# Two-layer graph network, layer 1: the exponential part of ELU taken as exp(-relu(-z)) on ScalarE and added by an accumulating DMA; the sum S1 of u formed by an accumulating load

## The chip, the cores and the metric

The kernel runs on one core of one Trainium2 chip. The metric is the device time of one execution in microseconds (us). The profile covers one execution; its span runs from the first to the last instruction of the core.

## The reference

16 graphs share one adjacency matrix of 1024 x 1024; each node has 512 features. Everything is float32.

```python
# layer 0
h = maximum(layernorm(x), 0)
x = x + (adj @ h) @ weight + bias                 # per graph
# layer 1
u = maximum(layernorm(x), 0)
h = u @ W
s1, s2 = h @ a[:512], h @ a[512:]
e = leaky_relu(s1[:, None] + s2[None, :], 0.2) * adj
att = softmax(e, axis=1)
x = x + elu(att @ h + beta * h)
```

elu(z) is max(z, 0) + min(exp(z), 1) - 1. Since min(exp(z), 1) = exp(min(z, 0)), it is also max(z, 0) + exp(-relu(-z)) - 1. The constant -1 is already in the stored residual x1, so a kernel adds relu and the exponential to x1 and nothing more.

## The kernel before

**Layers and batches.** Layer 0 is computed for the 16 graphs (the code calls them batches) one after another, then layer 1 for the 16. Layer 0 leaves three things of each batch in DRAM: the residual x1 (`x1d`, in four quarters by node half and by q), the normalised u (`ud`, tiles U00, U01, U10, U11) and the vectors for the logits. Layer 1 first forms z = p u, where p is the unnormalised softmax with beta on its diagonal, then multiplies by W (the tiles pq), and scales by 1/sum (`rs`) inside the ELU.

**Seven products.** Each 2 x 2 block product is done in seven products with sums of blocks (p1 to p7). S1, S2 and S4 are such sums on the left side; for layer 1 they are made from the four U tiles by `left_half`, called by `u_sums` in two parts: part 0 makes S1 (the sum of the right halves of U0q and U1q) and S2 = S1 - A11, part 1 makes S3 and S4. In layer 1 the second multiplication runs in the order p1, p5, p2, p6, p7, p3, p4 (`P5_EARLY`), each product in two halves q = 0, 1 of eight matmuls, in six PSUM banks: X (p5, p3), Y (p1, p6, p7, p4) and W (p2). p1's steps lie between the steps of the first multiplication's p4.

**The ELU.** When a product is finished, `done` copies or reads its bank. p6 and p5 are copied to z tiles by ScalarE (`part`); p7 and p3 are added to them by VectorE (`rest`), and then `elu` follows. p2 and p4 go to `elu` straight from PSUM. `elu(nh, oh, q, ...)` has `parts` (ScalarE: Relu into the output tile o, Exp into ez; each for two rows of 256 columns) and `total` (VectorE: o += min(ez, 1)). For p3 and p4 `total` is followed by a GpSimd DMA that adds x1 from DRAM to o, and `store` writes o out by SP's queue. ez is the z tile itself for p7 and p3, a tile of its own for p2 and p4; ez, z and the three `ext` tiles of the first multiplication's p4 share tag b2, which has five slots. o has tag xp with four slots, the U and S tiles tag up with seven.

**Order of the work.** Every instruction keeps its program order on its engine, and the same holds for the DMA queues of SP and GpSimd (POOL). Work beside the matmuls is placed by hand: plans map a step number k to functions. In the first multiplication step k comes after each half product (a step is 3.4 us) and k = 12 to 18 are the steps of its p4; in the second, k = 2n + q for product number n (1.7 us), to 13. What falls due later goes into the dictionary `later`, and a key over 13 becomes step key - 14 of the next batch. In layer 1 the softmax of the next batch runs beside the current batch: `masked` (M0 to M7, ScalarE and VectorE), `spread_max` (X, x: the row maxima out to DRAM and back, tiles md and mall, by SP), `top` (N, n), `exp` (E0 to E7, ScalarE), `turn` (V0 to V7, VectorE), `spread_sum` (S, s), `diagonal` (D, d). In batches 1 to 8 one row of batch 15's layer-0 output is also finished (`late`). In the profile nearly all lines are L119, that of the helper that keeps program order, so groups are told apart by tiles.

Of the kernel before, what the change touches and what calls it, by code (L numbers as in the profile page):

```python
# [29 lines left out]
F32 = mybir.dt.float32  # L30
AF = mybir.ActivationFunctionType
# [35 lines left out]
def kernel(  # L67
# [474 lines left out]
    def h_relu(b, k):  # L542
        h_norms.pop((b, k)).relu()

    def left_half(k, a11, a12, a21, a22, s, parts=(0, 1)):

        s1, s2, s4 = (s[n][:, ts(k, 2), :] for n in ("S1", "S2", "S4"))
        if 0 in parts:
            add(s1, a21, a22)
            add(s2, s1, a11, ALU.subtract)  # L550
        if 1 in parts:
            add(a21, a11, a21, ALU.subtract)
            add(s4, a12, s2, ALU.subtract)

    def h_sums(b, k):
        h1, h2 = hs[b, 0], hs[b, 1]
# [164 lines left out]
    def load_u(b, names):  # L721
        for n in names:
            t = uts.setdefault(b, {})[n] = up.tile([P, 2, D], F32, tag="up", name=f"ul_{b}_{n}")
            sp.dma_start(out=t.rearrange("p k d -> p (k d)"), in_=ud[b][n])

    def u_sums(b, q, part):
        t = uts[b]
        if q == 0 and part == 0:
            for n in ("S2", "S1", "S4"):
                t[n] = up.tile([P, HC, HD], F32, tag="up", name=f"ul_{b}_{n}")  # L730
        u1, u2 = t[f"U0{q}"], t[f"U1{q}"]
        left_half(q, u1[:, :, 0:HD], u2[:, :, 0:HD], u1[:, :, HD:D], u2[:, :, HD:D], t, (part,))

    def u_blk(b, n, k):
        t = uts[b]
# [6 lines left out]
    class Softmax:  # L742
# [9 lines left out]

        def logits(self):
            b = self.b
            self.rs = stat.tile([P, NCH], F32, tag="rs", name=f"rs_{b}")
            self.s1b = stat.tile([P, G, NCH], F32, tag="s1b", name=f"s1b_{b}", bufs=1)
            self.s2b = stat.tile([P, SN], F32, tag="s2b", name=f"s2b_{b}", bufs=1)
            for s in range(G):
                sp.dma_start(
                    out=self.s1b[ts(s, Q)], in_=s1d[b].rearrange("(t r) g -> r t g", r=Q)  # L760
                )
                sp.dma_start(
                    out=self.s2b[ts(s, Q)], in_=s2d[b][s, 0:SN].partition_broadcast(Q)
                )
# [92 lines left out]
        def diagonal(self, h):  # L857
            sz = stat.tile([P, 2, HC], F32, tag="sz", name=f"sz_{self.b}_{h}")
            dve.tensor_reduce(
                out=sz[:, 0, :], in_=self.half[h]["sall"].rearrange("p t i -> p i t"),  # L860
                axis=AX.X, op=ALU.add,
            )
            dve.reciprocal(self.rs[:, ts(h, HC)], sz[:, 0, :])
            dve.tensor_scalar(sz[:, 1, :], sz[:, 0, :], beta_c, None, op0=ALU.mult)
            for i in range(HC):
                d = self.t[f"B{h + 1}{h + 1}"][:, i, ts(i, P)]
                dve.scalar_tensor_tensor(
                    d, ident, sz[:, 1, i : i + 1], d, op0=ALU.mult, op1=ALU.add
                )
# [40 lines left out]
    def layer1(b, plan_a, plan):  # L910

        rs = sms[b].rs
        rows = node_rows(out, b)
        end = b == B - 1
        zs = {}
        sums = {}

        def elu(nh, oh, q, z, k):

            if end:  # L920
                r = b4.tile([P, 2, HD], F32, tag="b4", name=f"r_{b}_{nh}{oh}{q}")
            else:
                if (nh, q) not in sums:
                    sums[nh, q] = xp.tile([P, 2, D], F32, tag="xp", name=f"o_{b}_{nh}{q}")
                r = sums[nh, q][:, :, ts(oh, HD)]
            g0 = HC * nh + 2 * q
            ez = zs.pop((nh, oh, q), None)
            if ez is None:
                ez = b2.tile([P, 2, HD], F32, tag="b2", name=f"ez_{b}_{nh}{oh}{q}")

            def parts():
                for i in range(2):
                    sc = rs[:, g0 + i : g0 + i + 1]
                    act.activation(r[:, i, :], z[:, i, :], AF.Relu, scale=sc)
                    act.activation(ez[:, i, :], z[:, i, :], AF.Exp, scale=sc)

            if end or ez is not z:
                parts()
            else:
                later.setdefault(k + 1, []).append(parts)  # L940
            full = x1s[b, nh, q] if end else sums[nh, q]

            def total():
                d = full[:, :, ts(oh, HD)]
                if end:
                    add(d, d, r)
                dve.scalar_tensor_tensor(d, ez, 1.0, d, op0=ALU.min, op1=ALU.add)
                if nh != oh and not end:
                    pool.dma_start(
                        out=full.rearrange("p k d -> p (k d)"), in_=x1d[b][nh, q],  # L950
                        accum_op=ALU.add,
                    )

            def store():
                for s in range(G):
                    (act if end and nh and s % 2 else sp).dma_start(
                        out=rows[s][:, ts(2 * nh + q, 2), :], in_=full[ts(s, Q)]
                    )

            later.setdefault(k + (1 if end else 2 if ez is not z else 3), []).append(total)  # L960
            if nh != oh:
                later.setdefault(k + (1 if end else 7), []).append(store)

        products = NODES_LAST if end else P5_EARLY
        at = {p[0]: 2 * n for n, p in enumerate(products)}
        weighted1 = []

        def part(nh, oh, q, ps):
            zs[nh, oh, q] = b2.tile([P, 2, HD], F32, tag="b2", name=f"z_{b}_{nh}{oh}{q}")
            act.copy(zs[nh, oh, q], ps)  # L970

        def rest(nh, oh, q, ps, k):
            z = zs[nh, oh, q]
            add(z, ps, z)
            elu(nh, oh, q, z, k)

        def done(prod, q, ps):
            if prod == "p1":
                weighted1[0].fork("W", q, ps)
            elif prod == "p6":  # L980
                part(0, 1, q, ps)
            elif prod == "p5":
                part(1, 1, q, ps)
            elif prod == "p7":
                rest(1, 1, q, ps, at[prod] + q)
            elif prod == "p3":
                rest(0, 1, q, ps, at[prod] + q)
            else:
                elu(0 if prod == "p2" else 1, 0, q, ps, at[prod] + q)

        def after(k):
            for f in later.pop(k, ()):
                f()
            beside(plan)(k)

        weighted1.append(Weighted(f"pq{b}", w1_c, done, products))
        pT = sms[b].t

        def p4_operands():
            return partial(u_inner, b), p4_sums.pop(b), pT["T4"], p4_ext.pop(b)  # L1000

        beside(plan_a)(-1)
        left = products_a(
            f"z{b}", lambda n, k: u_blk(b, n, k), lambda n, k: pT[n][:, k, :], beside(plan_a),
            FORKED, p4=(p4_operands, weighted1[0]),
        )
        weighted1[0].rest(1, left, after)
# [77 lines left out]

    def logit_weights(k):

        v = stat.tile([P, DC], F32, tag="v", name=f"v_{k}")
        for dc in range(DC):
            dve.tensor_tensor_reduce(  # L1090
                out=junk(1), in0=w1_t[:, dc, :], in1=v_bcs[k], scale=1.0, scalar=0.0,
                op0=ALU.mult, op1=ALU.add, accum_out=v[:, dc : dc + 1],
            )
        vd[k] = dram.tile([D], F32, name=f"vd_{k}")
        sp.dma_start(out=vd[k].rearrange("(c p) -> p c", p=P), in_=v)
# [137 lines left out]
    for b in range(B):  # L1233
        plans = [plan_out(out_of, b)] if b else []
        plans_b = []
        if b + 1 < B:
            if b:
                plans.append(steps((-1, load_x, b + 1, 0), (-1, load_x, b + 1, 1)))
            plans.append(plan_norm_a(b + 1))
            out_of = LayerOut(b)  # L1240
            plans_b += [
                steps(
                    (11, out_of.stats, 0, 0, 0), (11, out_of.keep, 0, 0),
                    (12, out_of.stats, 0, 0, 1), (12, out_of.stats, 0, 1),
                ),
                plan_norm_b(b + 1), plan_softmax(EARLY_B.get(b, {}), sms[0]),
            ]
        else:
            plans.append(plan_softmax(FIRST_A, sms[0]))
            plans.append({  # L1250
                22: [(load_u, 0, ("U00", "U01"))], 25: [(load_u, 0, ("U10", "U11"))],
            })
            plans_b += [
                plan_softmax(FIRST_B, sms[0]), plan_softmax(LOGITS_B, sms[1]),
            ]
        if 0 < b <= G:
            plans.append({23: [(store_mask, b - 1)]})
# [22 lines left out]
    for b in range(B):  # L1280
# [24 lines left out]
            if b == NCH:  # L1305
                plan_b[13].append((late.store_logits,))
        if b + 1 < B:
            plan_b = merged(plan_b, steps((10, u_sums, b + 1, 0, 0), (12, u_sums, b + 1, 1, 0)))
        plans.append({18: plan_b.pop(1, [])})
        layer1(b, merged(*plans), plan_b)  # L1310
    for k in sorted(later):
# [35 lines left out]
```

## Time and profile before

| | |
|---|---|
| median of three runs | 2257.12 us (2254.89 to 2257.17) |
| the profiled execution's own time | 2254.63 us |
| its span | 2252.7 us |
| PE busy | 2236.1 us, 99% |
| VectorE busy | 1950.3 us, 87% |
| ScalarE busy | 1547.9 us, 69% |
| GpSimd busy | 243.7 us, 11% |
| DMA moved | 336.07 MB |

PE is TensorE's matmuls, ACT is ScalarE, DVE is VectorE, POOL is GpSimd, SP the queue of most DMAs. An instruction line in a timeline has its start, its duration, engine, line, operation, output <- inputs, shapes, count, and in brackets the idle time of the engine ahead of it and what ended it. A window's line has the busy time of each engine in that stretch, with the number of instructions in parentheses.

### The profile page before, as it was taken

The page shows a single profiled execution, that of the slowest core. Times are in us where ns is not written, and L with a number is a line of the kernel's source. Part 1 is how long each engine was busy: PE and PEld are TensorE (multiplying, and loading weights), DVE is VectorE, ACT ScalarE, POOL GpSimd, SP SyncE. Part 2 cuts the span into 40 slices and gives each one's busy share as a digit, 9 for nine tenths or more (in the row PEclk, how much of TensorE's full clock was granted, in tenths as well). Part 3 has the DMA queues.
Part 4 walks back from the last instruction along what each step waited for, and adds up shares of the span by engine and source line. Part 5 has one row for each costly group of instructions (what it writes and reads, how often), then busy time and mean ns, then how long its engine had stood idle before and what let it go on. Part 6 is the DMA issues. An engine that isn't in the chain of part 4 may idle for free.

```text
span 2252.7 us, 30436 instructions
## 1 busy us (share of the span) xinstructions
PE 2236.1 (99%) x8716; PEld 1645.5 (73%) x8716; DVE 1950.3 (87%) x4477; ACT 1547.9 (69%) x4138; POOL 243.7 (11%) x508
## 2 busy tenths in 40 slices
PE   9999999999999999999999999999999999999998
PEld 5888888888888888888666556665666556665565
DVE  7888888998888998898989988898889988888864
ACT  3766766676777676776576777768777776767743
POOL 1211111111111111111000000000000000000000
PEclk9999999999999999999999999999999999999999
DMA  7433454443444343344535665465554655446541
GB/s 210 140 126 119 160 171 132 141 140 117 148 160 151 134 142 120 120 150 159 202 110 175 165 169 166 145 196 156 164 168 149 191 142 153 139 143 165 159 120 49
DMA packets 194296, 336.07 MB, mean 149 GB/s; under 512 B 78800, under 2 KB 86992, under 8 KB 194128
## 3 DMA queue, kind: packets, MB, share of 16 engines
q1 hardware_dynamic: 185168, 302.15, 41.2%
q0 software_dynamic: 8640, 31.46, 7.5%
q8 instruction: 68, 1.11, 0.2%
q14 instruction: 100, 0.82, 0.1%
q10 hardware_dynamic: 320, 0.52, 0.1%
HBM read 228.33 MB, written 109.91 MB: 150 GB/s over the span
## 4 chain that ended last, share of the span: by engine, by line
PE 96%; DVE 2%; ACT 1%; DMA 1%; issue 0%; POOL 0%; SPq 0%; DVEq 0%; POOLq 0%
PE z_Y L119 16%; PE po_Y L119 10%; PE pq_Y L119 9%; PE z_X L119 9%; PE y_Y L119 8%; PE po_X L119 5%; PE z_W L119 5%; PE pq_X L119 5%; PE y_X L119 4%; PE y_W L119 3%; PE y_p7y L119 2%; PE pq_W L119 2%; PE po_W L119 2%; PE z_p4y L119 2%; PE y_p3y L119 2%; PE y_p4y L119 2%
## 5 line engine op out<-in xcount | busy, mean ns | idle before, releaser
L119 ACT ACTIVATE e<-e,nm 128x256 f32<-128x256 f32 x480 | 236.8, 498 | 51.4 <-DVE nm L119 51.4
L119 DVE CUSTOM_DVE_ANT_0 e<-e,mask 128x256 f32<-128x256 f32 x512 | 199.9, 424 | 54.0 <-ACT e L119 52.8
L119 PE MATMUL z_Y<-pT,ul_U 128*128 128x512 f32 x512 | 224.9, 592 | 0.0
L119 ACT ACTIVATE e<-s2b,s1b 128x256 f32<-128x256 f32 x512 | 214.7, 500 | 0.0
L119 PE MATMUL pq_Y<-w_c,z_C 128*128 128x256 f32 x768 | 189.1, 379 | 0.0
L119 PE MATMUL po_Y<-w_c,y_C 128*128 128x256 f32 x768 | 188.3, 379 | 0.0
L119 PEld LDWEIGHTS z_Y<-pT,ul_U 128*128 128x128 f32 x512 | 97.3, 190 | 115.6 <-issue 111.5
L119 DVE CUSTOM_DVE_ANT_0 y_S<-xr,v_bc 128x512 f32<-128x512 f32 x240 | 165.3, 689 | 9.2 <-DVE s L119 0.5
L119 PEld LDWEIGHTS po_Y<-w_c,y_C 128*128 128x128 f32 x768 | 145.9, 190 | 20.3 <-ACT po_X L119 0.2
L119 PEld LDWEIGHTS pq_Y<-w_c,z_C 128*128 128x128 f32 x768 | 145.9, 190 | 19.9
L119 DVE STREAM_TRANSPOSE pT<-e 128x512 f32<-128x512 f32 x240 | 150.8, 680 | 1.5
L119 ACT ACTIVATE h<-h,nb_h,r_h 128x512 f32<-128x512 f32 (+1 forms) x132 | 98.2, 792 | 57.1 <-POOL nb_h L119 57.1
L119 ACT ACTIVATE y_S<-xr 128x512 f32<-128x512 f32 x90 | 56.7, 630 | 91.9 <-DVE xr L119 91.5
L119 POOL DMA_DIRECT2D o<-x1d x60 | 52.7, 935 | 609.7 <-DVE o L119 546.8
L119 PE MATMUL pq_X<-w_c,z_S 128*128 128x256 f32 x512 | 115.9, 379 | 0.0
L119 PE MATMUL po_X<-w_c,y_S 128*128 128x256 f32 x512 | 115.7, 379 | 0.0
L119 PE MATMUL z_W<-pT,ul_U 128*128 128x512 f32 x256 | 112.5, 592 | 0.0
L119 PE MATMUL z_Y<-pT_T,ul_S 128*128 128x512 f32 x256 | 112.5, 592 | 0.0
L119 PE MATMUL z_X<-pT_T,ul_S 128*128 128x512 f32 x256 | 112.5, 592 | 0.0
L119 PE MATMUL z_X<-pT,ul_S 128*128 128x512 f32 x256 | 112.5, 592 | 0.0
L119 PEld LDWEIGHTS pq_X<-w_c,z_S 128*128 128x128 f32 x512 | 96.3, 190 | 14.5 <-DVE z_C L119 0.8
L119 PEld LDWEIGHTS po_X<-w_c,y_S 128*128 128x128 f32 x512 | 97.3, 190 | 13.2
(259 smaller groups left out, 5238.3 us busy)
## 6 DMA issues: line engine op xcount, KB each, us to landing
mask<-maskd SPq DMA_DIRECT2D x128, 512.0 KB
h<-in_x_dram SPq DMA_DIRECT2D x64, 512.0 KB
xr<-in_x_dram SPq DMA_DIRECT2D x256, 128.0 KB
x1d<-xr SPq DMA_DIRECT2D x64, 512.0 KB
ul_U<-ud_U SPq DMA_DIRECT2D x64, 512.0 KB
ud_U<-xr SPq DMA_DIRECT2D x60, 512.0 KB
o<-x1d POOLq DMA_DIRECT2D x60, 512.0 KB, 8.0
out_dram<-o SPq DMA_DIRECT2D x240, 128.0 KB
```

Source lines behind the costliest of these rows:

```text
L119: return lambda *args, **kwargs: tc.keep_in_program_order(f(*args, **kwargs))
```

## The change

In batches 0 to 14 of layer 1, `parts` makes ez with two Relu of scale -1/sum (a second half of `rs` that GpSimd fills) and one Exp of scale -1 over 512 columns in place. Two DMAs on GpSimd's queue follow from `parts` itself: o += ez, and for p3 and p4 o += x1. VectorE's `total` and its place in `later` go. The last batch keeps Exp, `total` and its steps. S1 of each batch is no longer added by VectorE: `load_s1` has SP load the right half of U0q from DRAM and GpSimd's queue add that of U1q, at step 2 of the batch before (for batch 0 at step 5 of layer 0's last batch). The tag of a small tile used once (`v`) is shared with another.

```diff
+    def load_s1(b):
+        s1 = up.tile([P, HC, HD], F32, tag="up", name=f"ul_{b}_S1")
+        uts.setdefault(b, {})["S1"] = s1
+        for i, queue in ((0, sp), (1, pool)):
+            for q in range(2):
+                queue.dma_start(
+                    out=s1[:, ts(q, 2), :],
+                    in_=ud[b][f"U{i}{q}"].rearrange("p (k d) -> p k d", d=D)[:, :, HD:D],
+                    **({"accum_op": ALU.add} if i else {}),
+                )
...
     def u_sums(b, q, part):
...
-            for n in ("S2", "S1", "S4"):
+            for n in ("S2", "S4"):
...
-        left_half(q, u1[:, :, 0:HD], u2[:, :, 0:HD], u1[:, :, HD:D], u2[:, :, HD:D], t, (part,))
+        if part == 0:
+            add(t["S2"][:, ts(q, 2), :], t["S1"][:, ts(q, 2), :], u1[:, :, 0:HD], ALU.subtract)
+        else:
+            left_half(q, u1[:, :, 0:HD], u2[:, :, 0:HD], u1[:, :, HD:D], u2[:, :, HD:D], t, True)
...
-            dve.reciprocal(self.rs[:, ts(h, HC)], sz[:, 0, :])
+            dve.reciprocal(self.rs[:, 0, ts(h, HC)], sz[:, 0, :])
+            pool.tensor_scalar(
+                self.rs[:, 1, ts(h, HC)], self.rs[:, 0, ts(h, HC)], -1.0, 1.0, op0=ALU.mult,
+                op1=ALU.mult,
+            )
...
+            full = x1s[b, nh, q] if end else sums[nh, q]
+
             def parts():
                 for i in range(2):
-                    sc = rs[:, g0 + i : g0 + i + 1]
-                    act.activation(r[:, i, :], z[:, i, :], AF.Relu, scale=sc)
-                    act.activation(ez[:, i, :], z[:, i, :], AF.Exp, scale=sc)
+                    c = slice(g0 + i, g0 + i + 1)
+                    act.activation(r[:, i, :], z[:, i, :], AF.Relu, scale=rs[:, 0, c])
+                    if end:
+                        act.activation(ez[:, i, :], z[:, i, :], AF.Exp, scale=rs[:, 0, c])
+                    else:
+                        act.activation(ez[:, i, :], z[:, i, :], AF.Relu, scale=rs[:, 1, c])
+                if end:
+                    return
+                act.activation(ez, ez, AF.Exp, scale=-1.0)
+                pool.dma_start(out=r, in_=ez, accum_op=ALU.add)
+                if nh != oh:
+                    pool.dma_start(
+                        out=full.rearrange("p k d -> p (k d)"), in_=x1d[b][nh, q],
+                        accum_op=ALU.add,
+                    )
...
             def total():
                 d = full[:, :, ts(oh, HD)]
-                if end:
-                    add(d, d, r)
+                add(d, d, r)
                 dve.scalar_tensor_tensor(d, ez, 1.0, d, op0=ALU.min, op1=ALU.add)
-                if nh != oh and not end:
-                    pool.dma_start(
-                        out=full.rearrange("p k d -> p (k d)"), in_=x1d[b][nh, q],
-                        accum_op=ALU.add,
-                    )
...
-            later.setdefault(k + (1 if end else 2 if ez is not z else 3), []).append(total)
+            if end:
+                later.setdefault(k + 1, []).append(total)
...
-            plan_b = merged(plan_b, steps((10, u_sums, b + 1, 0, 0), (12, u_sums, b + 1, 1, 0)))
+            plan_b = merged(plan_b, steps(
+                (2, load_s1, b + 1), (10, u_sums, b + 1, 0, 0), (12, u_sums, b + 1, 1, 0)
+            ))
```

More of the change, by code (lines that the diff above doesn't have):

```diff
@@ L543, in h_relu, with left_half @@
         h_norms.pop((b, k)).relu()
-    def left_half(k, a11, a12, a21, a22, s, parts=(0, 1)):
+    def left_half(k, a11, a12, a21, a22, s, rest=False):
         s1, s2, s4 = (s[n][:, ts(k, 2), :] for n in ("S1", "S2", "S4"))
-        if 0 in parts:
+        if not rest:
             add(s1, a21, a22)
             add(s2, s1, a11, ALU.subtract)
-        if 1 in parts:
-            add(a21, a11, a21, ALU.subtract)
-            add(s4, a12, s2, ALU.subtract)
+        add(a21, a11, a21, ALU.subtract)
+        add(s4, a12, s2, ALU.subtract)
     def h_sums(b, k):
@@ L754, in logits @@
             b = self.b
-            self.rs = stat.tile([P, NCH], F32, tag="rs", name=f"rs_{b}")
+            self.rs = stat.tile([P, 2, NCH], F32, tag="rs", name=f"rs_{b}")
             self.s1b = stat.tile([P, G, NCH], F32, tag="s1b", name=f"s1b_{b}", bufs=1)
@@ L940, in elu @@
                 later.setdefault(k + 1, []).append(parts)
-            full = x1s[b, nh, q] if end else sums[nh, q]
             def total():
                 d = full[:, :, ts(oh, HD)]
-                if end:
-                    add(d, d, r)
+                add(d, d, r)
                 dve.scalar_tensor_tensor(d, ez, 1.0, d, op0=ALU.min, op1=ALU.add)
-                if nh != oh and not end:
-                    pool.dma_start(
-                        out=full.rearrange("p k d -> p (k d)"), in_=x1d[b][nh, q],
-                        accum_op=ALU.add,
-                    )
             def store():
@@ L1086, in logit_weights @@
     def logit_weights(k):
-        v = stat.tile([P, DC], F32, tag="v", name=f"v_{k}")
+        v = stat.tile([P, DC], F32, tag="bn", name=f"v_{k}")
         for dc in range(DC):
@@ L1254 @@
                 plan_softmax(FIRST_B, sms[0]), plan_softmax(LOGITS_B, sms[1]),
+                steps((5, load_s1, 0)),
             ]
```

## The prediction

> **What bounds the kernel now.** I read the busy shares first, then who keeps TensorE waiting, then one batch of layer 1 engine by engine.
>
> ```profile
> PE 2236.1 (99%) x8716; PEld 1645.5 (73%) x8716; DVE 1950.3 (87%) x4477; ACT 1547.9 (69%) x4138; POOL 243.7 (11%) x508
> 1314.29:1385.75 71.46, 71.46 (x237) 44.70 (x237) 62.95 (x158) 51.92 (x149) 5.32 (x8) 1.00 0.59 166
> 1110.00:1160.00 50.00, 48.76 (x157) 29.35 (x156) 47.37 (x115) 32.99 (x104) 0.00 (x0) 1.00 0.43 145
> ```
>
> The second and third lines are windows (length, then busy time of PE, PEld, DVE, ACT, POOL, then clock, DMA share, GB/s). A layer-1 batch takes 71.4 us and PE is busy in all of it; VectorE has 8.5 us to spare in a batch, ScalarE 19.5. In layer 1 only batch 0 (third line) shows PE idle, 1.24 us. The other idle time of PE, 16.6 us in all, is 4.2 us in the first 25 us, 10.0 us in the last 63, and about 1 us elsewhere; the change touches neither end. So work taken from VectorE can return about 1 us, and the question is only whether the new path makes PE wait. The matmul spans are modelled, but their starts are regular: 16 of 256 columns every 3.45 us, all through layer 1. What PE needs, and when, stands in the timeline of batch 3:
>
> ```profile
> 1368.32 3.62 PE L119 MATMUL pq_W<-w_c,z_C 128*128 128x256 f32 x16
> 1371.77 3.62 PE L119 MATMUL pq_Y<-w_c,z_S 128*128 128x256 f32 x16
> 1375.22 3.62 PE L119 MATMUL pq_Y<-w_c,z_C 128*128 128x256 f32 x16
> 1392.45 7.03 PE L119 MATMUL z_W<-pT,ul_U 128*128 128x512 f32 x16
> ...
> 1370.29 0.47 ACT L119 ACTIVATE o<-pq_W,rs 128x256 f32<-128x256 f32 x1 [1.19 <-DMA s2b<-s2d]
> 1373.70 0.59 ACT L119 COPY z<-pq_Y 128x512 f32<-128x512 f32 x1
> 1375.42 0.59 ACT L119 COPY z<-pq_Y 128x512 f32<-128x512 f32 x1 [1.14 <-PE pq_Y L119]
> 1378.30 0.51 ACT L119 ACTIVATE o<-z,rs 128x256 f32<-128x256 f32 x1 [2.29 <-DVE z L119]
> 1382.70 0.81 ACT L119 ACTIVATE late<-late,nb_u,r_u 128x512 f32<-128x512 f32 x1 [0.54 <-POOL nb_u L119]
> 1390.06 0.61 ACT L119 COPY z_W<-z_Y 128x512 f32<-128x512 f32 x1
> ```
>
> p2, p6 and p7 of the weighted product follow one another; p6 and p7 accumulate in the same two Y banks, so p7's second half (8 matmuls on, 1376.95) must wait for ScalarE's copy of p6's second half, which ends at 1376.01: **0.94 us of slack**. The copy into z_W ends at 1390.67 and p2 of the next batch uses it at 1392.45: **1.78 us of slack** where a late batch-15 row is handled (b = 1 to 8), 2.66 us where not (1817.72 + 0.57 against 1820.95). These are the two places where ScalarE can stop PE.
>
> **What the skill says.** "DMA: Bandwidth & Descriptors", SWDGE vs HWDGE vs iDMA: accumulation is possible from GpSimd's queue alone. The trace agrees: o<-x1d, the one accumulating transfer, is POOL's. The same page, Anatomy of one DMA — SWDGE (gpsimd) path, prices one at 2.0 us plus bytes over 436 GB/s: 3.2 us for 512 KB, 2.6 us for 256 KB. The trace differs:
>
> ```profile
> 1388.00 0.91 POOL L119 DMA_DIRECT2D o<-x1d  x1 [5.33 <-DVE o L119]
> DMA to landing us min/median/max: 5.6/5.6/5.6
> o<-x1d POOLq DMA_DIRECT2D x60, 512.0 KB, 8.0
> ```
>
> The one issued at 1388.00 runs alone on idle DMA engines and lands after 5.6 us; all 60 have a median of 8.0. The trace decides. Queues, rings and completion order: an engine with several rings turns between them packet by packet; here the transfers that overlap mask loads are the long ones (9.4 us for that of 1395.46), which agrees. "ScalarE: Activation LUTs", Table sets: relu is in exp's set; the profile has one table load in the whole span, so no reload is charged.
>
> **The change, part by part** (batches 0 to 14 of layer 1; the last keeps its code).
>
> *VectorE.* Eight scalar_tensor_tensor of 0.69 us a batch go (the groups o<-ez,o and o<-z,o, 120 in all), and two S1 adds of 0.68 us: 6.9 us a batch, some 103 us in all. PE covers it wholly: gain 0 to 1.2 us, taken as 0.
>
> *ScalarE.* Each of eight parts keeps four 128x256 instructions (Exp becomes Relu, both near 0.47 to 0.51 us) and gets one Exp of 128x512 in place. No row has it. From 256 to 512 columns a PSUM copy goes from 0.37 to 0.586 us, so 0.50 for an Exp of 256 gives 0.71; back to back the spans overlap by 0.1, so 0.62 of queue time. Bounds: 0.5 and 0.8 (the scaled 128x512 row of xr). That is 5.0 us a batch beside 19.5 idle: it matters only ahead of the two copies.
>
> *The wait for the slot (step 1).* Tag b2 has five slots. When p6's second half is to be copied out, z of p5 (two tiles, in use until p7) and z of p6's first half are held, and so are both ez of p2. Before, the sixth tile took the slot of p2's first ez as soon as VectorE had read it (1373.67 to 1374.36). Now that slot is free only when the DMA r += ez has landed. From PE's end of p2's first half (1370.2): 0.1 to ScalarE, 1.57 for four Relu, 0.13 for the wait on its own result, 0.71 for Exp, 0.1 to POOL, then the landing L, 0.1, the copy 0.59, 0.1 to PE: 3.4 + L. PE wants it 6.75 us after 1370.2. So PE stalls L - 3.35. L for 256 KB in 1 KB pieces has no row: alone, first packet 1.6 us after issue (as at 1388.00), half of the 2.6 us of packets, and the 1.4 left of the 5.6: 4.3. Four mask loads (2 MB, issued from 1370.6) share the engines until 1378; the contended 512 KB takes 1.4 to 3.8 us longer than the lone one. I take L = 6.5, bounds 4.2 and 9.4. Stall 3.15 us, bounds 0.85 and 6.05; times 15 batches: **47 us** (13 to 91). Behind the waiting copy on ScalarE stand p7's parts, which wait for VectorE's add anyway.
>
> *ScalarE's lag at z_W (step 2).* After that stall ScalarE begins p7's first part 1.5 us late, PE is 3.15 late. Six parts add 6 x 0.62 = 3.7 us, of which ScalarE's old 0.54 and part of its 2.29 us wait absorb some; the late row's POOL steps now stand behind the DMA issue of p7's first part (0.9 us). Worked through, the z_W copy lands some 1.1 us past its need in eight batches and 0.3 in seven: **11 us**. If step 1 is short the absorption goes and this grows to 1.8 and 0.9, 21 us; with a long one it is nothing.
>
> *POOL and SP (step 3).* POOL gets eight r DMAs and two S1 DMAs a batch at 0.9 us of issue, and two small tensor_scalar (0.3 us). For p3 and p4 it waits, in order, for r to land before it may issue o += x1d; the next half's r stands behind. With landings of 4 to 8 us this is a chain of four links, about 28 to 35 us from p3's first part to the last landing, where before four transfers went out within 7.5. SP waits for each with its stores, and behind the third store is the second max exchange (md, then mall), at 1414.96 before. By my times that is issued about 4 us later, with PE 4 us later too: 0 taken. ScalarE has no idle time between 1413.84 and 1431, and the p4 copies in it have about 1.2 us to spare, so each us beyond that stops PE: bounds 0 and 4 us a batch, 60 us.
>
> *S1 by transfer.* Two SP loads (0.4 us each to issue, ahead of the logit and mask loads, which have 20 us before their use) and two accumulating ones which wait for them on POOL. Issued about 1364, landed about 1374; VectorE uses S1 at 1381.2. Cost 0; if it were 5 us late VectorE's 8.5 us of idle, now 15, covers it. Its packets are done before p2's r DMA starts; if not, L takes it up.
>
> **Sum.** 2254.6 us is the profiled execution's own time (its span 2252.7, with 1.9 around it). 47 + 11 + 0 = 58 gives 2312.6; the median is 2.5 us above that execution, so 2315.
>
> **Rivals.**
> (B) *POOL's chain decides as well*: landings of 8 us or more put the second max exchange over 1.2 us behind PE. For it: the median of 8.0, and SP already waited 8.6 us at most for a small md transfer. Against: the four o += x1d no longer run on top of each other. 2 to 4 us more in 15 batches: 2345 to 2375.
> (C) *Short landing*: L about 4.3, stall 0.95, and the z_W lag of 1.8 and 0.9: 15 x 0.95 + 21 = 35, so 2292. Against: the mask loads at that moment.
> (D) *Not slower*: the transfer is hidden at p6's second copy. It decides at L = 3.35 us; below that PE sees nothing there, and if ScalarE's extra Exp costs under 0.3 us a part (1.78 over six) z_W is in time too: 2256, about 1 us under. Against: a first packet at 1.6 us and 1.4 us to land leave 0.35 for the packets. That the change should not do what it says I see no way for: the two VectorE groups are gone from the code.
>
> **Numbers.** 0.2% is about 4.5 us, what a measurement of this kernel can tell from no change. Forecast (A) 0.52, B 0.25, C 0.15, D 0.08, of which 0.05 within 0.2% and 0.03 faster. A alone spans 2295 to 2345; the range takes in C's lower bound (13 + 11) and B: 2278 to 2380.
>
> **What would show it.** Right: PE idle ahead of p7's second half in each of 15 batches, released by ScalarE's z copy, that copy waiting for a DMA on o; a smaller one at z_W; 120 Exp of 128x512 near 0.71 us; VectorE down by about 103 us; landing of o<-ez near 6.5. Wrong: a batch still at 71.4 us (D), or PE's largest idle in p4 or at the softmax (B), or a stall released by S1.

## The result, and the profile after

The changed kernel takes **2473.09 us** (median of four runs, 2466.22 to 2473.38) against 2256.01 us for the kernel before, measured beside it: a ratio of 1.0955, 95% interval 1.0934 to 1.0975. It is slower, as forecast, but by 217 us where 58 were forecast: far outside the range.

The profiled execution has a span of 2464.3 us, 211.6 more than before. From the page of the kernel after, the busy shares and GpSimd's DMA queue (packets, MB, share of the DMA engines' time; before it had 8640 packets):

```profile
PE 2306.4 (94%) x8716; PEld 1681.5 (68%) x8716; DVE 1860.4 (75%) x4325; ACT 1618.4 (66%) x4258; POOL 438.1 (18%) x692
...
q0 software_dynamic: 49984, 71.32, 18.0%
```

PE's idle time rose from 16.6 us to 157.9. Its busy time rose too, by 70.3 us, though it does the same 8716 matmuls. Both parts have to be explained. PE's list of waits in the kernel after (us in all, times, longest):

```profile
PE z_p4y L119 <- ACT z_p4t L119: 71.7, 15, 5.9
PE pq_Y L119 <- ACT z L119: 69.5, 14, 7.4
PE z_W L119 <- ACT z_W L119: 2.5, 6, 1.0
```

Two waits of like size, each once a batch: the second line is step 1 of the prediction (p7's second half, 47 us forecast), the third is step 2 (11 us forecast). The first, at p4 of the next batch's first multiplication, is the place of step 3, which was taken at nothing. PE's timeline shows both waits in one batch:

```profile
1675.73 1.94 PE L119 MATMUL pq_Y<-w_c,z_C 128*128 128x256 f32 x8
1685.11 3.57 PE L119 MATMUL pq_Y<-w_c,z_C 128*128 128x256 f32 x8 [7.45 <-ACT z L119]
...
1739.63 0.59 PE L119 MATMUL pq_Y<-w_c,z_C 128*128 128x256 f32 x2
1746.11 2.08 PE L119 MATMUL z_p4y<-ext,in 128*128 128x256 f32 x4 [5.89 <-ACT z_p4t L119]
```

The same eight matmuls take 1.94 us before the wait and 3.57 after it; four matmuls of p4 take 2.08 us where such a group takes 1.03. Slow groups like these, behind nearly every such wait, are most of the 70 us of extra busy time: by PE's starts 59 us are lost while the clock is down, and some 8 us in small delays elsewhere. The windows around the first wait (length, then busy time of PE, PEld, DVE, ACT and POOL, then the granted clock, DMA share, GB/s) say why:

```profile
1678.00:1681.00 3.00, 0.00 (x0) 0.00 (x0) 0.45 (x1) 0.00 (x0) 0.00 (x0) 1.00 1.02 295
1681.00:1684.00 3.00, 0.00 (x0) 0.00 (x0) 0.00 (x0) 0.00 (x0) 0.00 (x0) 0.58 1.03 227
1684.00:1687.00 3.00, 1.89 (x5) 1.53 (x6) 0.00 (x0) 2.43 (x6) 0.00 (x0) 0.50 0.10 16
```

The granted clock falls to one half while PE waits, and PE begins again at half speed. Nothing of this stands in the prediction.

**Why p7 waits.** ScalarE's timeline, at p6's two copies:

```profile
1675.05 0.57 ACT L119 COPY z<-pq_Y 128x512 f32<-128x512 f32 x1
1684.47 0.58 ACT L119 COPY z<-pq_Y 128x512 f32<-128x512 f32 x1 [8.86 <-DMA o<-ez]
```

The second copy waits for the first r += ez to land, as step 1 has it (r is the part of o that this ELU writes, so the profile calls the transfer o<-ez). That transfer was issued at 1673.33 and landed after 11.1 us. Over the first of each batch, 0 to 13, the landings are 5.6 to 11.1 us, mean 8.5; in batch 14, where no mask is loaded, it is 3.8. What the DMA queues moved says what held it (packets, MB, share of the 16 engines; q1 is SP's queue, q0 GpSimd's; the first pair is 1675 to 1678 us, the second 1681 to 1684):

```profile
q1 hardware_dynamic: 246, 0.91, 99.8%
q0 software_dynamic: 1, 0.00, 0.2%
...
q0 software_dynamic: 358, 0.34, 71.7%
q1 hardware_dynamic: 102, 0.34, 31.8%
```

Four mask loads of 512 KB were issued by SP from 1672.74 on. For three microseconds they have the engines to themselves: GpSimd's queue moves one packet. What it moved before 1675 was the tail of the S1 transfers; the packets of r += ez come after 1677.5, mixed with the masks'.

**Why p4 waits.** The chain runs back from ScalarE's p4 copy through its Exp (e, of the softmax) and VectorE's nm to the max exchange. ScalarE, then VectorE:

```profile
1739.80 0.51 ACT L119 ACTIVATE e<-e,nm 128x256 f32<-128x256 f32 x1 [6.13 <-DVE nm L119]
...
1745.71 0.35 ACT L119 COPY z_p4t<-z_p4y 128x256 f32<-128x256 f32 x1
```

```profile
1739.30 0.26 DVE L119 TENSOR_REDUCE nm<-mall 128x16 f32<-128x64 f32 x1 [6.25 <-DMA mall<-md]
```

ScalarE has 5.9 us of Exp ahead of the copy in its program order, and none of it can start without nm. SP's queue, first in the kernel before, then in the kernel after (the second duration is that of twelve stores):

```profile
1409.25 5.61 SPq L119 DMA_DIRECT2D out_dram<-o  x12
1414.96 0.39 SPq L119 DMA_DIRECT2D md<-mx  x1
```

```profile
1720.34 13.00 SPq L119 DMA_DIRECT2D out_dram<-o  x12
1733.45 0.46 SPq L119 DMA_DIRECT2D md<-mx  x1
```

In this batch SP nowhere waits over 0.35 us among the stores. It is the issuing that takes long: up to 1.85 us for one store. Of the 240 stores of o, 48 take over 0.8 us to issue and every one of these has an accumulating transfer of GpSimd's in flight (so have two thirds of the quick ones); in the kernel before there are seven, up to 2.0 us, five of them with one in flight. The median is 0.43 us in both. Medians over the 14 batches with this exchange, from the same rows: from the first store to md 9.6 us against 5.8, of which 7.9 against 5.0 is issuing and the rest waits for landings; the first store itself leaves 17.5 us ahead of p4 where it left 18.5; and from md's issue to the p4 copy there are 1.5 us more. So md leaves 7.7 us ahead of p4, not 12.6, and the copy ends some 6.4 us later against PE's work. These 14 waits are 70.5 us, 5.0 each, which leaves 1.4 us of former slack; the fifteenth, in batch 0, is 1.2 us and was there before.

### The profile page after: what moved, and what is told of

It reads as the page before. It is cut to its first block, busy times and chain, and to the rows that moved or that the text cites. A ratio compares the mean times of both kernels' runs of the same rounds, so it can differ in the third digit from the quotient of the medians.

```text
span 2464.3 us, 30821 instructions
## 1 busy us (share of the span) xinstructions
PE 2306.4 (94%) x8716; PEld 1681.5 (68%) x8716; DVE 1860.4 (75%) x4325; ACT 1618.4 (66%) x4258; POOL 438.1 (18%) x692
## 5 line engine op out<-in xcount | busy, mean ns | idle before, releaser
L119 PE MATMUL pq_Y<-w_c,z_C 128*128 128x256 f32 x768 | 225.0, 429 | 69.7 <-ACT z L119 69.5
L119 PEld LDWEIGHTS pq_Y<-w_c,z_C 128*128 128x128 f32 x768 | 164.5, 218 | 105.1 <-ACT z L119 78.4
L119 DVE TENSOR_TENSOR z<-pq_Y,z 128x512 f32<-128x512 f32 x32 | 22.1, 691 | 148.1 <-PE pq_Y L119 112.2
L119 PE MATMUL z_p4y<-ext,in 128*128 128x256 f32 x128 | 46.8, 501 | 71.7 <-ACT z_p4t L119 71.7
L119 PEld LDWEIGHTS pq_X<-w_c,z_S 128*128 128x128 f32 x512 | 101.9, 199 | 16.3 <-DVE z_C L119 0.6
```

The costliest lines, as they stand in the source:

```text
L119: return lambda *args, **kwargs: tc.keep_in_program_order(f(*args, **kwargs))
```

## The experiments

Two theories stood at the start. **Theory**: two separate chains, the b2 slot (p7) and the stores ahead of the max exchange in SP's queue (p4), each with the half-speed matmuls that follow a wait. **Rivals**: one cause for both (GpSimd's queue as such, or ScalarE's extra Exp), or the S1 load. Each ratio below is against the kernel before, run beside it.

**The b2 slot alone.** p2's two ez get one tile of tag b4; p6's copies then find a free b2 slot.

```diff
-                ez = b2.tile([P, 2, HD], F32, tag="b2", name=f"ez_{b}_{nh}{oh}{q}")
+                if nh == 0 and not end:
+                    if q == 0:
+                        ezs[0] = b4.tile([P, 2, 2, HD], F32, tag="b4", name=f"ez_{b}_{nh}{oh}")
+                    ez = ezs[0][:, q]
+                else:
+                    ez = b2.tile([P, 2, HD], F32, tag="b2", name=f"ez_{b}_{nh}{oh}{q}")
```

> The changed kernel with p2's two ez tiles in one b4 tile of their own, so that p6's second copy finds a free b2 slot; nothing else changed. Theory (two separate waits, each with a stretch of slowed TensorE clock behind it): the gap ahead of p7's second half (69.5 us in 14 waits) goes to zero, with some 30 us of slow matmuls behind it, so about 2370 us; the p4 gap stays near 5 us a batch. Rival (the DMA engines are overloaded, and a wait taken away at one place comes back at the next): above 2430 us, p4's gap or z_W's grows by about 5 us a batch. Rival (ScalarE's extra Exp is what is late): p7's gap stays.

Measured 2386.48 us, ratio 1.0577 (1.0562 to 1.0593). PE's waits:

```profile
PE z_p4y L119 <- ACT z_p4t L119: 68.2, 15, 6.8
PE z_W L119 <- ACT z_W L119: 17.5, 15, 2.0
```

The wait at p7 is gone, that at p4 stays, and step 2 appears at its forecast size for a short step 1 (17.5 against 21 us). The span falls by 79.0 us: 69.5 of wait at p7 and 3.5 at p4, less 15.0 that z_W takes back, and 21.8 of PE's busy time, mostly of half-speed matmuls (the median of the runs falls by 86.6).

**The stores alone.** p3's and p4's stores fall due three steps later, behind the second max exchange.

```diff
-                later.setdefault(k + (1 if end else 7), []).append(store)
+                later.setdefault(k + (1 if end else 10), []).append(store)
```

> The changed kernel with the stores of o three steps later, so that they stand behind the second max exchange in SP's queue. Theory: that exchange no longer waits for POOL's chain; the p4 gap (71.7 us in 15 waits) and about 33 us of slow matmuls behind it go, 2370 us; p7's gap stays at about 5 us a batch. Rival (small transfers land late because the DMA engines are full): md lands 7 us after its issue as before, p4's gap falls by less than half, above 2425 us. Rival (ScalarE's lag from the extra Exp makes the p4 copies late): no change, 2473 us.

Measured 2407.22 us, ratio 1.0675 (1.0659 to 1.0691).

```profile
PE pq_Y L119 <- ACT z L119: 108.8, 15, 11.1
PE z_p4y L119 <- ACT z_p4t L119: 2.1, 3, 1.8
```

The wait at p4 is gone, so it came through the order in SP's queue: the slow stores, and GpSimd's chain of transfers behind them, no longer stop PE there once md stands ahead of them. The time missed the expectation, because the wait at p7 grew by 39 us. Its transfer is issued later: 2.4 us after its Exp on average, against 0.35 in the kernel after. SP, with its stores moved, comes to the S1 loads later; GpSimd's two accumulating S1 loads wait for these, and r += ez stands behind them in the same queue. GpSimd's timeline in batch 2, where the Exp ends at 1317.06:

```profile
1319.24 2.24 POOL L119 DMA_DIRECT2D ul_S<-ud_U  x2 [6.93 <-DMA ul_S<-ud_U]
1320.74 1.98 POOL L119 DMA_DIRECT2D o<-ez  x1
```

Over 15 batches the later issue is some 31 of the 39 us. The rest is the landing, 7.2 to 12.0 us in batches 0 to 13, mean 9.0 against 8.5. So S1's load costs a second time here, by its place in GpSimd's queue.

**Both.** The two edits together.

> Both edits together. Theory: both gaps gone, no slowed clock in layer 1, what is left is ScalarE's lag at z_W of 0 to 25 us: 2256 to 2285 us. Rival (overloaded DMA engines): a new gap, above 2320 us.

Measured 2290.33 us, ratio 1.0155 (1.0135 to 1.0175).

```profile
PE z_W L119 <- ACT z_W L119: 18.4, 15, 2.0
PE z_p4y L119 <- ACT z_p4t L119: 2.2, 2, 1.5
```

Two edits of order and buffers take away 183 of the 217 us, 5 us less than the expected range allows. Most of what is left is ScalarE at z_W: 18.4 of the 32.8 us by which the span exceeds that of the kernel before. The slowed clock was to be gone and is not quite: behind the longest of these waits 5 us of slow matmuls are left.

**The masks out of the way.** The four mask loads are held behind S2, which VectorE writes at step 10, after p7, by a small load that SP issues ahead of them.

```diff
+    held = dram.tile([1, 16], F32, name="held")
+
+    def hold(b):
+        sp.dma_start(out=held, in_=uts[b]["S2"][0:1, 0, 0:16])
...
-    LOGITS_B = {8: "L", 9: "L0", 10: "L1", 11: "e2", 12: "e3"}
+    LOGITS_B = {8: "L", 13: "L0 L1 e2 e3"}
...
+            plan_b = merged(steps((10, hold, b + 1)), plan_b)
+            plan_b[10] = plan_b[10][1:] + plan_b[10][:1]
```

> The changed kernel with the four mask loads of p2's time held in SP's queue until VectorE has made S2 of the next batch (a 64-byte transfer out of S2 stands ahead of them), some 10 us later. Theory (the mask loads, queued first, starve the accumulating transfer): p2's first o<-ez lands in 4 to 6 us instead of 11.1, p7's gap falls to 1 or 2 us a batch and the slow clock behind it goes: 2380 to 2400 us. Rival (the two accumulating S1 loads ahead of it in POOL's queue delay it): it still lands after 8 us or more, 2460 us. If the masks then come late for the next softmax, VectorE waits for them and p4's gap grows.

Measured 2430.93 us, ratio 1.0773 (1.0757 to 1.0789).

```profile
PE z_p4y L119 <- ACT z_p4t L119: 111.5, 15, 11.5
PE z_W L119 <- ACT z_W L119: 10.0, 8, 1.6
PE pq_Y L119 <- ACT z L119: 5.6, 8, 1.6
```

With no mask load near it, the first r += ez lands after 3.8 to 5.2 us in all fifteen batches, and the wait at p7 falls from 69.5 to 5.6 us: the masks are what stretched the landing. The time was missed because the masks now meet the later transfers, the stores wait longer for them (13.2 to 17.5 us from the first store to md), and p4 waits 40 us more. Here moving the load did not remove the contention; it changed who paid.

**S1 by transfer, alone and left out.** The first kernel is the one before with `load_s1` and its S1 adds removed; the second is the one after with S1 added by VectorE again.

```diff
-            for n in ("S2", "S4"):
+            for n in ("S2", "S1", "S4"):
...
+            add(t["S1"][:, ts(q, 2), :], u1[:, :, HD:D], u2[:, :, HD:D])
...
-                steps((5, load_s1, 0)),
...
-                (2, load_s1, b + 1), (10, u_sums, b + 1, 0, 0), (12, u_sums, b + 1, 1, 0)
+                (10, u_sums, b + 1, 0, 0), (12, u_sums, b + 1, 1, 0)
```

> The kernel before with the accumulating load of S1 alone. Theory: free, since VectorE was not what TensorE waited for and S1 lands before it is read: 2255 us, within 0.2%. Rival (the S1 transfers delay the mask loads or the p4 stage): over 2262 us, with idle time of TensorE released by S1, a mask or a p4 copy.

> The changed kernel with S1 added by VectorE as before, so the ELU part alone. Theory: the two waits stay; since the S1 loads also hold SP's mask loads back by some 1.7 us into the time of p2's first o += ez, the p7 gap falls by up to that: 2430 to 2475 us. Rival (POOL's S1 transfers are a main cause of the late landing): the first o<-ez lands in under 7 us and the p7 gap goes, under 2400 us.

Alone, the load costs nothing large: 2256.93 us, ratio 1.0008 (1.0002 to 1.0015). Without it the changed kernel takes 2422.51 us, 1.0744 (1.0726 to 1.0763), which lies between the theory and its rival. So in company the load costs 51 us:

```profile
PE z_p4y L119 <- ACT z_p4t L119: 65.6, 15, 5.7
PE pq_Y L119 <- ACT z L119: 36.4, 15, 4.7
```

The wait at p7 is halved; the first r += ez lands after 6.1 us on average in batches 0 to 13. In the kernel after, S1's transfers fill the engines just ahead of it and hold the masks back into its time.

**ScalarE's part alone.** The kernel before with the changed `parts` (two Relu, one Exp of 512 columns), and VectorE adds ez as it did.

```diff
+                    c = slice(g0 + i, g0 + i + 1)
+                    act.activation(r[:, i, :], z[:, i, :], AF.Relu, scale=rs[:, 0, c])
...
+                        act.activation(ez[:, i, :], z[:, i, :], AF.Relu, scale=rs[:, 1, c])
+                if not end:
+                    act.activation(ez, ez, AF.Exp, scale=-1.0)
...
+                    add(d, d, ez)
```

> The kernel before with ScalarE's new form (two Relu of each sign and one Exp of 512 columns) but VectorE adding ez to o as it did, and o += x1 issued as before; no accumulating transfer of ez, S1 as before. Theory: only ScalarE's lag is left, at the z_W copy: 1 to 2 us a batch after batches with a late row and 0 to 1 after the others, 2265 to 2285 us. Rival (the lag in the run with both edits comes from POOL's steps or the transfers): 2256 us and no gap at z_W.

Measured 2275.55 us, ratio 1.0089 (1.0073 to 1.0104): 20.6 us without any new transfer.

```profile
PE z_W L119 <- ACT z_W L119: 11.8, 15, 1.1
PE z_p4y L119 <- ACT z_p4t L119: 2.6, 1, 2.6
```

The first line is step 2 by itself. The second is batch 0 alone (1.2 us in the kernel before); the clock falls there, for 1.7 us of slow matmuls. Most of the rest of the 20.6 us is in starts spread by a few tenths, which the modelled ends count as busy.

**p4's last part later.** On top of both edits, p4's second part of ScalarE work goes behind the z_W copy.

```diff
+            if not end and nh and not oh and q:
+                later.setdefault(k + 2, []).append(parts)
-            if end or ez is not z:
+            elif end or ez is not z:
```

> The run with both edits (own tile for p2's ez, stores later), and p4's second half of the ELU put two steps later, behind both z_W copies of the next batch. Theory (ScalarE's queue ahead of z_W is the last wait): the z_W gap goes and the time is that of before, 2254 to 2260 us, not below, since TensorE is then busy throughout. Rival: the later part pushes the next copies, and a gap appears at p6 or p5 of the first multiplication: still over 2275 us.

Measured 2283.63 us, ratio 1.0126 (1.0112 to 1.014): the theory missed. z_W does get better, but not by the full amount, and VectorE has a new wait for sall (4.8 us in 6 waits with both edits alone). PE's wait, then VectorE's:

```profile
PE z_W L119 <- ACT z_W L119: 8.8, 6, 4.4
```

```profile
DVE sz L119 <- DMA sall<-sd: 41.3, 19, 3.6
DVE ul_S L119 <- DMA ul_S<-ud_U: 28.1, 15, 4.6
```

sd and sall are the exchange of the row sums, again behind stores in SP's queue. SP's timeline there:

```profile
1878.06 9.74 SPq L119 DMA_DIRECT2D out_dram<-o  x8
1887.91 0.38 SPq L119 DMA_DIRECT2D sd<-sm  x1
```

The second line of VectorE's waits, S1 landing late, is another candidate, so both were tried.

**The last stores past the sums, with and without the S1 load.** In batches 0 to 13 (the code's b < B - 2; the expectation says 12) p4's stores fall due six steps later; the second kernel also adds S1 on VectorE, by the edit shown above.

```diff
-                later.setdefault(k + (1 if end else 10), []).append(store)
+                later.setdefault(k + (1 if end else 16 if nh and b < B - 2 else 10), []).append(store)
```

> As e9_both_p4_part_later, and the two stores of p4's half (nh = 1) fall due six steps later, past both exchanges of the row sums (sd, then sall), in batches 0 to 12. Theory (SP's order once more): in e9 those stores hold sd and sall back, VectorE waits for sall (41.3 us in 19 waits against 4.8 in 6 without the later part), so its add for p7 and ScalarE's z_W copy behind it are late. With the stores out of the way that wait falls to about 5 us, TensorE's wait for z_W to under 3 us, and the time to 2256 to 2268. Rival 1 (S1): VectorE's lateness is its wait for S1's accumulating load (28.1 us in 15 waits in e9): then sall's wait falls and the time stays near 2280. Rival 2 (the instruction count): ScalarE's extra work is what is left; then z_W stays at 9 us or more and the time at 2275 to 2285.

> As e10_last_stores_past_sums, with S1 added by VectorE again instead of by the accumulating load. If S1's load costs nothing once the other orders are mended, this is within 4 us of e10. If VectorE's wait for S1 is what keeps e10 above the kernel before, this one is near 2256 to 2260 and e10 10 us or more above it. If VectorE's 1.4 us a batch that the load took away matter, this one is the slower of the two.

Measured 2274.39 us, ratio 1.0081 (1.0065 to 1.0098), and 2267.66 us, 1.0055 (1.004 to 1.007). In the first, VectorE's wait for sall falls to 4.4 us in 5 waits, as the theory had it; its wait for S1 stays, at 27.8 us in 12. The second has neither. PE's waits, the first kernel, then the second:

```profile
PE z_W L119 <- ACT z_W L119: 11.8, 6, 2.9
PE z_p4y L119 <- ACT z_p4t L119: 3.0, 4, 2.0
```

```profile
PE z_p4y L119 <- ACT z_p4t L119: 5.4, 5, 1.8
```

The first missed the theory in its time: moving the stores won 9 us, and z_W still waits. Without the S1 load no wait at z_W is left, so that load was its cause there, worth 6.7 us. That it acts by VectorE's wait for S1 (the add ahead of p7's part stands behind it) fits the two lists, but the run also takes the load's packets and its place in GpSimd's queue away. The second kernel missed its 2256 to 2260 us too. The last kernel is the best form found and is still 0.4 to 0.7% slower than the kernel before, with ScalarE 65.6 us busier than before. Of its 12.8 us, 4.2 are the line above (5.4, less the 1.2 of the kernel before), and by PE's starts about 9 are gaps under 0.6 us each, which the kernel before has not. That the rest of ScalarE's work causes these is likely, not shown.

## Why the prediction was wrong, point by point

**What bounds the kernel: right.** PE was the bound and VectorE's relief returned nothing: 89.9 us less of busy time (103 forecast) bought no time that any run shows.

**Step 1, the wait for the slot: mechanism right, one term mis-sized.** PE's wait was to be L - 3.35 a batch. With the measured mean of 8.5 us over 14 batches that gives 72 us; PE's wait is 69.5. In the kernel without the S1 load L is 6.1 and the same sum gives 39; measured 36.4. So the formula holds and L = 6.5 was the term. In the run with the stores moved it needs one term more, the later issue, which the prediction took at 0.1 us. The bound of 9.4, the landing of one contended transfer of the kernel before, held the mean, but six of the fourteen lie above it. The prediction let the mask loads and r += ez share the engines, with the Trainium skill's page "DMA: Bandwidth & Descriptors", Queues, rings and completion order, where an engine's rings take turns packet by packet. The same section gives the size of a turn: a whole packet, typically 9 to 17 descriptors. In the three microseconds in which q0 got one packet, q1 moved 246, 15 for each of the 16 engines. If a packet of the profile is a descriptor of the page, that is one long turn, and the two agree; no run tests it. The kernel before has it the other way round: of the mask loads issued from 1392.78 us on, nothing moved until 1396.5, while GpSimd's queue moved 207 packets. The lone landing, estimated at 4.3 us, was good: 3.8.

**The S1 load at cost 0: right alone, wrong in company.** "If not, L takes it up" was the right sentence, and it was given no number. It was 2.4 us of L in each of 14 batches: 33 us of wait, 51 us of time.

**Step 2, ScalarE's lag at z_W: mechanism right.** 11 us were forecast and 2.5 measured, because step 1 was longer, and with a long step 1 it was to vanish. For a short step 1 21 us were forecast; in the runs without the p7 wait z_W waits 17.5 and 18.4 us, and ScalarE's part by itself costs 20.6 us of time, 11.8 of it as this wait. The Exp of 128x512 takes 0.63 us, not 0.71. From the tile's view of the kernel after, the Exp and the landings of p2's and p4's r += ez (those of p7 and p3, which stand there as o<-z, have a median of 3.8):

```profile
L119 ACT ACTIVATE ez<-ez x60: 629/630/632, 1157.8 to 2388.7; 128x512 f32<-128x512 f32 x60
...
DMA to landing us min/median/max: 3.8/7.6/11.1
```

**Step 3, POOL and SP: the step that failed outright.** It was taken at 0 with a bound of 4 us a batch; it is 5.0. The prediction named the place (the stores ahead of md, then nm, ScalarE's Exp, the p4 copy) and its slack (1.2 us; 1.4 measured). It argued that SP would be about 4 us late with PE 4 us late too. That part came true: the first store leaves 17.5 us ahead of p4, nearly as before. What it didn't price is what follows the first store: twelve issues at 0.43 us were taken as they were, and they cost 2.9 us more; md's own way to the p4 copy, 1.5 us more, which was not taken apart. Rival B had the right consequence and part of the mechanism, since waits for landings are only about 1 us of it. GpSimd's issue of an r += ez takes 1.2 to 1.3 us (medians), not 0.9.

**No term for the clock.** After the two waits the matmuls run at half speed, 59 us by their starts, over a third of the error and as much as the whole forecast. The Trainium skill's page "TensorE: Matmul & The Clock Gate", Part 1, says it: half clock "after ≥1 idle window (~3.4µs)", in a window that runs freely. The traces of the eleven changed kernels show the same with a lower edge, and there they decide. Counted by how late PE's next matmul starts, none of 63 waits of 0.6 to 1.9 us in layer 1 is followed by a lowered clock, 15 of 27 of 1.9 to 3.2 us are (from 2.1 us on), and all 89 longer ones are, with 1.5 to 3.2 us of extra time each. A forecast stall of 3.15 us a batch, with a bound of 6.05, should have carried that term.

Summed up for the 211.6 us of span: 22.5 more at p7 than forecast, 70.5 at p4, 8.5 less at z_W, and 70.3 of busy time make 154.8 us, against the 153.6 by which the forecast's 58 fell short.

## What to carry to other kernels

Work moved from a busy engine to DMA is not off the path as long as a buffer, or a queue with an exchange in it, waits for the transfer: list who needs the slot, what stands behind each store and what stands ahead of each transfer in its own queue, and price the landing with all the traffic of that moment, the change's own other transfers included. A stall of TensorE beyond two to three microseconds must be charged again for the half-speed matmuls after it. Where a change loses at several places, undo them together: each mended alone, the next wait took back part of the gain or grew (the stores alone 66 us, the slot alone 87, both 183).

## What the runs showed of the hardware that was not expected

- An accumulating transfer of 256 KB on GpSimd's queue lands after 3.8 us on idle DMA engines and after up to 11.1 us when 2 MB of loads are in SP's queue: in 1675 to 1678 us q1 had 99.8% of the engines. With the loads moved away it lands after 3.8 to 5.2 us.
- SP took up to 1.85 us, in one batch 2.5, to issue one store while GpSimd's transfers ran, against a median of 0.43; issues over 0.8 us went from 7 to 48 of 240. That the two compete for something is likely from the times, but no run isolates it.
- The granted clock falls to 0.50 in 15 of the 27 waits of PE of 1.9 to 3.2 us (the shortest is 2.1), and in all 89 longer ones.
